# A coupled-map lattice on TensorE: six channels in groups of three with rings of 80 rows, regrouped into pairs with rings of 56 rows on two row tiles

## The chip, the cores and the metric

The kernel runs on one core of a Trainium2 chip. The metric is the device time of one execution in microseconds (us). All arithmetic concerned here is 32-bit floating point.

Words used below: *PE* or TensorE is the engine of matrix products, *DVE* is VectorE, *ACT* is ScalarE, *POOL* is GpSimd, *SP* is SyncE, which here only issues transfers. A *queue* is the list of instructions of one engine, which runs in order.

## The reference

Four layers, each of the form `x = x + f(group_norm(x))`, on 32 images of 8 channels and 256 x 256 pixels. The change concerns the first layer alone, and in it the map that is iterated 15 times:

```python
drive = x[:, :C_OUT]                       # all 8 channels, normalised
grid = drive
for _ in range(STEPS):                     # 15
    mapped = R * grid * (1.0 - grid)
    local = _conv(mapped, K_local, groups=C_OUT)      # 3x3, each channel by itself
    physics = (1.0 - EPS) * mapped + EPS * local
    grid = (1.0 - BETA) * physics + BETA * drive
cml_out = jnp.clip(grid, 0.0001, 1.0 - 0.0001)
h = jax.nn.relu(_conv(x, Wp, bp))                     # 3x3, 8 -> 128
nca_out = jax.nn.sigmoid(_conv(h, Wu, bu))            # 1x1, 128 -> 8
gin = jnp.concatenate([x, cml_out, nca_out], axis=1)
g = jax.nn.sigmoid(_conv(jax.nn.relu(_conv(gin, Wg1, bg1)), Wg2, bg2))
return g * cml_out + (1.0 - g) * nca_out
```

Layers 2 to 4 are a quantised 3x3 convolution, a 3x3 convolution and a 5x5 box filter; nothing of them is changed.

## The kernel before, in words

**Stages.** The first layer takes the first 13.6 ms of the span, one image (*batch*) after another. Layers 2 to 4 are pipelined over the batches in the rest.

**The map.** Six of the eight channels are iterated on TensorE, the other two on VectorE. For TensorE an image is cut into 32 x 16 patches of 8 columns by 16 rows. The 128 pixels of a patch lie on the 128 partitions, and the 512 patches lie along the free axis. So one step of a channel is one product with a 128 x 128 matrix (`patch_sb`, L391: all neighbours inside the patch) plus one product for the neighbours that lie in other patches: the *ring*. The table `RINGS` tells which pixels of which neighbouring patch are needed. The function `spread` (L250) copies those rows of the state, shifted by one patch, into the tile `rings`, and a second product (`ring_sb`, L393) adds their part in the same accumulator. The ring has 80 rows: 16 for the left side, 16 for the right, and 24 for the top and 24 for the bottom (8 pixels times three patches, the patches to the left and right included, of which most weights are zero).

**A step, in halves.** The channels are in two halves of three (`HALF`), each with its own tile of states and of rings. A half is: three patch products (L391), three ring products (L393), then on VectorE three additions of the drive in the accumulator (L402, 128 x 512), and on ScalarE three squares (L419) that write the new state; then `spread` issues four transfers on SP's queue (L259), which write `rings` for the next step. The accumulators come from a pool `ps_c` of three buffers of 512 columns, so a patch product has to wait until the square three products earlier has read its buffer.

**The two channels on VectorE.** Their image lies in `strip`; `tap` (L338) is one multiply-add of 128 x 1024 elements, nine of them a step: three in the first half, six in the second, followed by a maximum (L412) and the map itself (L413), which writes `strip`. Then `edges` copies the rows that neighbouring partitions need, with two transfers on SP's queue (L263, L264). VectorE's queue is in order, so a half's additions stand behind the taps of the half before.

**What lies between.** The rest of the layer (the hidden convolution, and the gate) for the batch before is a generator, `gated` (L487), whose pieces are put between the pieces of the map by hand. `lattice` yields a number at each place where other work may stand, and the main loop (L664 to L671) draws pieces of `gated` until their own numbers have used it up. A piece may be a product `ph` (L633) with its ReLU on ScalarE (L638), a group of four products `pn` (L610, each 32 columns wide, on column tiles), or gate products (L531, L539, L543, L548). Behind a gate's products come seven operations on VectorE (L561 to L568). A half yields 1.7 after its additions and taps, then issues squares and transfers, and yields `BLOCK - 1.7`, with `BLOCK = 6.3`. The statistics and the loads of the next batch come from a third generator, `errands` (L266), one piece a half; its transfers and those of `gated` are on POOL's queue. The first batch has no batch before it, so its steps have no such work between. All queues keep the order in which the program is written (`manual_schedule`).

Of the kernel before, what the change touches and what calls it, by code (L numbers as in the profile page):

```python
# [9 lines left out]
F32 = mybir.dt.float32  # L10
BF16 = mybir.dt.bfloat16
AF = mybir.ActivationFunctionType
ALU = mybir.AluOpType
# [4 lines left out]
P = 128  # L18
# [3 lines left out]
RB = H // HB  # L22
# [14 lines left out]
RINGS = (  # L37
    (0, 16, PW - 1, PW, -SY, 1, 0),
    (16, 16, 0, PW, SY, 1, 0),
    (32, 8, (RB - 1) * PW, 1, -1 - SY, 3, SY),  # L40
    (56, 8, 0, 1, 1 - SY, 3, SY),
)
RING = 80


CP = 6
HALF = CP // 2
RQ = 4
BLOCK = 6.3
STEPS = 15  # L50
R_, EPS_, BETA_ = 3.9, 0.3, 0.15

# [8 lines left out]
def window(ap, offset, dims):  # L61

    return bass.AP(ap.tensor, ap.offset + offset, [list(d) for d in dims])
# [3 lines left out]
def kernel(  # L67
# [10 lines left out]
    def const(pool, src, shape, name):  # L78
        t = pool.tile(shape, F32, name=name)
        nc.sync.dma_start(t, src)  # L80
        return t
# [86 lines left out]
    with ExitStack() as es:  # L168
# [6 lines left out]
        psum = es.enter_context(tc.tile_pool(name="ps_a", bufs=3, space=PSUM))  # L175

        patch_sb = const(wt, patch, [P, CP, P], "patch_sb")
        ring_sb = const(wt, ring, [RING, CP, P], "ring_sb")
        taps_sb = const(wt, taps, [P, 9], "taps_sb")
        kern_sb = const(wt, kern, [P, CP, 9], "kern_sb")  # L180
        pick_sb = const(wt, pick, [P, P], "pick_sb")
# [37 lines left out]
        d2s = [wt.tile([P, RQ, W], F32, name=f"d2_{i}") for i in range(2)]  # L219
        nh = wt.tile([P, 8, WP], F32, name="nh")  # L220
        zero = wt.tile([C, WP], F32, name="zero")
        states = [wt.tile([P, HALF, SN], F32, name=f"state{i}") for i in range(2)]
        rings = [wt.tile([RING, HALF, SN], F32, name=f"rings{i}") for i in range(2)]
        flat = wt.tile([P, NPX], F32, name="flat")
        acc = wt.tile([P, RQ, W], F32, name="acc")
        sts = [[wt.tile([P, 2], F32, name=f"st{j}_{i}") for j in range(2)] for i in range(2)]
        strip = wt.tile([P, RQ + 2, WP], F32, name="strip")
        for t in (*xbs, nh, zero, strip):
            nc.gpsimd.memset(t, 0.0)
        for t in (*states, *rings):  # L230
            nc.gpsimd.memset(t, 0.25)


# [11 lines left out]

        def inner(c):

            return states[c // HALF][:, c % HALF, AT : AT + TX * SY].rearrange("p (x y) -> p x y", y=SY)[:, :, 0:TY]

        def spread(half):  # L250

            long = (HALF - 1) * SN + RN
            state = states[half]
            row = state.ap[0][0]
            to = rings[half].rearrange("p c n -> p (c n)")
            for q, n, p, step, far, m, by in RINGS:
                at = p * row + AT + far
                dims = [[step * row, n]] + ([[by, m]] if m > 1 else []) + [[1, long]]
                nc.sync.dma_start(to[q : q + n * m, 0:long], window(state, at, dims))  # L259

        def edges():

# [65 lines left out]
        def lattice(b, ahead):  # L328
# [8 lines left out]
            def tap(dy, dx):  # L337
                nc.vector.scalar_tensor_tensor(  # L338
                    acc, strip[:, dy : dy + RQ, dx : dx + W],
                    taps_sb[:, 3 * dy + dx : 3 * dy + dx + 1],  # L340
                    d2 if dy == 1 and dx == 0 else acc, ALU.mult, ALU.add,
                )
# [27 lines left out]
                    edges()  # L370
                yield 1
            dr = flat.rearrange("p (x c y) -> p c x y", x=TX, c=C)
            for c in range(CP):
                nc.scalar.activation(inner(c), dr[:, c], AF.Square, bias=minus)
                nc.scalar.activation(
                    dr[:, c], dr[:, c], AF.Identity, bias=lift[:, c : c + 1], scale=BETA_
                )
                if c == 0:
                    nc.scalar.mul(d2, d2, BETA_)
                if c % HALF == HALF - 1:  # L380
                    spread(c // HALF)
                yield 1.5
            yield 4
            for step in range(STEPS):
                for half in range(2):
                    mine = range(HALF * half, HALF * half + HALF)
                    pss = []
                    for c in mine:
                        ps = ps_c.tile([P, 512], F32, name="psc")
                        pss.append(ps.rearrange("p (x y) -> p x y", y=TY))  # L390
                        nc.tensor.matmul(pss[-1], patch_sb[:, c, :], inner(c), start=True, stop=False)  # L391
                    for c in mine:
                        nc.tensor.matmul(  # L393
                            pss[c % HALF], ring_sb[:, c, :],
                            rings[half][:, c % HALF, 0 : TX * SY].rearrange(
                                "p (x y) -> p x y", y=SY
                            )[:, :, 0:TY],
                            start=False, stop=True,
                        )
                    for c in mine:  # L400
                        ps = pss[c % HALF]
                        nc.vector.scalar_tensor_tensor(ps, ps, FLOOR, dr[:, c], ALU.max, ALU.add)  # L402
                    if step == STEPS - 1:
                        for c in mine:
                            nc.vector.tensor_scalar(
                                dr[:, c], pss[c % HALF], 0.0001, 1.0 - 0.0001, ALU.max, ALU.min
                            )
                    for dy in (1,) if half == 0 else (0, 2):
                        for dx in range(3):
                            tap(dy, dx)  # L410
                    if half == 1 and step < STEPS - 1:
                        nc.vector.tensor_scalar(acc, acc, FLOOR, None, ALU.max)  # L412
                        nc.vector.scalar_tensor_tensor(own, acc, 1.0, acc, ALU.subtract, ALU.mult)  # L413
                    if half == 1 and step == STEPS - 1:
                        nc.vector.tensor_scalar(own, acc, 0.0001, 1.0 - 0.0001, ALU.max, ALU.min)
                    yield 1.7
                    if step < STEPS - 1:
                        for c in mine:
                            nc.scalar.activation(inner(c), pss[c % HALF], AF.Square, bias=minus)  # L419
                        spread(half)  # L420
                        if half == 1:
                            edges()
                    next(ahead, None)
                    yield BLOCK - 1.7
            for t4 in range(TX // 4):
                ps = psum.tile([P, 512], F32, name="ps")
                for j in range(4):
# [481 lines left out]
def laid_out(inputs):  # L909
# [6 lines left out]
    w3h = np.zeros((72, 2, P), f)  # L916
    k5 = inputs["L3_conv_weight"][0, 0]
    patch = np.zeros((P, CP, P), f)
    ring = np.zeros((RING, CP, P), f)
    for m in rows:  # L920
        for dy in range(3):
            for dx in range(3):
                y, x = m // PW + dy - 1, m % PW + dx - 1
                far = (-SY if x < 0 else SY if x >= PW else 0) + (-1 if y < 0 else y >= RB)
                p = y % RB * PW + x % PW
                if far == 0:
                    patch[p, :, m] = K[:CP, 0, dy, dx]
                for q, n, p0, step, far0, count, by in RINGS:
                    for j in range(count):
                        i, off = divmod(p - p0, step)  # L930
                        if far0 + j * by == far and off == 0 and 0 <= i < n:
                            ring[q + i * count + j, :, m] = K[:CP, 0, dy, dx]
    for dy in range(5):
        for m in rows:
            k = m + dy - 2
# [107 lines left out]
```

## Time and profile before

| | us |
|---|---|
| median of 3 runs (16277.27 to 16305.33) | 16303.53 |
| the profiled execution | 16318.33 |
| its span, first to last instruction | 16316.6 |

| engine, share of the span busy | |
|---|---|
| TensorE products (42888) | 95% |
| TensorE weight loads | 38% |
| VectorE | 72% |
| ScalarE | 35% |
| GpSimd | 34% |
| mean granted clock of TensorE | 0.961 |

| group | count | mean of one |
|---|---|---|
| L391 patch product, 128 x 512 | 5760 records | 626 ns |
| L393 ring product, 80 rows, 512 columns | 5760 records | 607 ns |
| L402 addition on VectorE | 2880 | 696 ns |
| L338 tap on VectorE | 4320 | 1284 ns (with `acc`), 1277 ns (with `d`) |
| L413 the map on VectorE | 448 | about 1227 ns |
| L419 square on ScalarE | 2688 | 690 ns |
| L259 ring transfer of 159.5 KB, and of 106.3 KB | 1920 each | |
| L263, L264 transfers of `strip`, 126 KB | 960 | |

How to read it. A product of 32-bit numbers is two records of TensorE, one after the other, each with its own weight load; so 5760 records are 2880 products (32 batches x 15 steps x 6 channels). Records overlap in time, so their mean length is more than what each one costs; the distance from start to start tells the cost. The DMA engines are busy for 67% between the first and the last batch of the first layer, VectorE for 76%.

### The profile page before, as it was taken

The page shows a single profiled execution, that of the slowest core. Times are in us where ns is not written, and L with a number is a line of the kernel's source. Part 1 is how long each engine was busy: PE and PEld are TensorE (multiplying, and loading weights), DVE is VectorE, ACT ScalarE, POOL GpSimd, SP SyncE. Part 2 cuts the span into 40 slices and gives each one's busy share as a digit, 9 for nine tenths or more (in the row PEclk, how much of TensorE's full clock was granted, in tenths as well). Part 3 has the DMA queues.
Part 4 walks back from the last instruction along what each step waited for, and adds up shares of the span by engine and source line. Part 5 has one row for each costly group of instructions (what it writes and reads, how often), then busy time and mean ns, then how long its engine had stood idle before and what let it go on. Part 6 is the DMA issues. An engine that isn't in the chain of part 4 may idle for free.

```text
span 16316.6 us, 141125 instructions
## 1 busy us (share of the span) xinstructions
PE 15452.2 (95%) x42888; PEld 6215.7 (38%) x42888; DVE 11705.9 (72%) x14652; ACT 5726.7 (35%) x8862; POOL 5598.2 (34%) x9491
## 2 busy tenths in 40 slices
PE   6999999999999999999999999999999997999999
PEld 2333333333333333333333333333333332333333
DVE  7777777777777777777777777777777764555554
ACT  2433444443434434443434444343444442111110
POOL 1333333333333333333333333333333342111111
PEclk7999999999999999999999999999999998999999
DMA  4766666666666666666666666666666664555554
GB/s 104 148 146 144 150 147 144 147 150 146 149 144 148 150 147 147 144 147 145 147 142 149 148 144 147 141 148 146 147 149 147 146 134 98 119 119 119 119 118 105
DMA packets 1057742, 2276.12 MB, mean 139 GB/s; under 512 B 419740, under 2 KB 623508, under 8 KB 1050724
## 3 DMA queue, kind: packets, MB, share of 16 engines
q0 software_dynamic: 704512, 1492.80, 40.6%
q1 hardware_dynamic: 352484, 774.29, 23.4%
q8 instruction: 356, 5.83, 0.2%
q14 instruction: 390, 3.19, 0.1%
HBM read 1078.04 MB, written 471.38 MB: 95 GB/s over the span
## 4 chain that ended last, share of the span: by engine, by line
PE 74%; DVE 13%; DMA 7%; ACT 3%; issue 2%; SPq 1%; POOL 0%; DVEq 0%; ACTq 0%; POOLq 0%
PE ph L633 17%; PE psc L391 14%; PE psc L393 13%; PE pg L531 9%; DVE acc L338 7%; PE psv L725 5%; PE pn L610 5%; PE psv L811 4%; DMA qb<-qh 3%; DMA rings<-state 2%; PE psv L729 2%; PE pq L548 1%; PE pg L543 1%; PE pg L539 1%; DVE psc L402 1%
## 5 line engine op out<-in xcount | busy, mean ns | idle before, releaser
L338 DVE SCALAR_TENSOR_TENSOR acc<-strip,taps_sb,acc 128x1024 f32<-128x1024 f32 x3840 | 4930.4, 1284 | 124.8 <-DMA strip<-strip 4.7
L505 POOL DMA_DIRECT2D im<-xn_d x6144 | 3458.3, 566 | 3250.0 <-PE ph L633 1434.7
L633 PE MATMUL ph<-im,wp_sb 72*128 72x512 f32 x8192 | 4091.7, 615 | 308.8 <-ACT hh L638 251.3
L638 ACT ACTIVATE hh<-ph,bp_sb 128x512 f32<-128x512 f32 x4096 | 2755.8, 690 | 4441.9 <-PE ph L633 4385.7
L402 DVE SCALAR_TENSOR_TENSOR psc<-psc,flat 128x512 f32<-128x512 f32 x2880 | 1921.4, 696 | 2813.0 <-PE psc L393 2797.2
L391 PE MATMUL psc<-state,patch_sb 128*128 128x512 f32 x5760 | 2812.0, 626 | 74.1 <-ACT state L419 63.3
L393 PE MATMUL psc<-rings,ring_sb 80*128 80x512 f32 x5760 | 2713.5, 607 | 129.8 <-DMA rings<-state 129.8
L633 PEld LDWEIGHTS ph<-im,wp_sb 72*128 72x128 f32 x8192 | 1489.5, 193 | 2425.4 <-issue 1587.8
L419 ACT ACTIVATE state<-psc,minus 128x512 f32<-128x512 f32 x2688 | 1690.2, 690 | 1818.8 <-DVE psc L402 1713.1
L391 PEld LDWEIGHTS psc<-state,patch_sb 128*128 128x128 f32 x5760 | 1114.5, 199 | 1696.2 <-issue 1375.7
L393 PEld LDWEIGHTS psc<-rings,ring_sb 80*128 80x128 f32 x5760 | 1114.7, 194 | 1576.8 <-issue 1545.7
L569 POOL DMA_DIRECT2D x_d<-xc x256 | 146.9, 574 | 3493.1 <-DVE xc L564 3416.6
L811 PE MATMUL psv<-xr,w_sb 128*128 128x512 f32 x2560 | 1162.9, 600 | 1.3 <-DVE xr L792 1.3
L610 PE MATMUL pn<-hh,wu_sb 128*32 128x512 f32 x8192 | 1133.9, 609 | 3.3 <-ACT hh L638 3.3
L776 POOL DMA_DIRECT2D x_d<-x x512 | 321.0, 643 | 1941.0 <-DVE x L770 1696.3
L725 PE MATMUL psv<-xh,w_sb 128*128 128x512 f32 x1536 | 753.0, 629 | 9.6 <-issue 9.6
L531 PE MATMUL pg<-xq,wg_sb 128*128 128x512 f32 x1536 | 749.3, 626 | 0.0
L754 ACT ACTIVATE x<-psv,b_sb,sc 128x512 f32<-128x512 f32 x256 | 199.3, 779 | 1466.2 <-PE psv L729 1465.8
L531 PE MATMUL pg<-cq,wg_sb 128*128 128x512 f32 x1536 | 713.7, 601 | 0.0
L811 PEld LDWEIGHTS psv<-xr,w_sb 128*128 128x128 f32 x2560 | 466.1, 189 | 610.8 <-issue 606.0
L338 DVE SCALAR_TENSOR_TENSOR acc<-strip,taps_sb,d 128x1024 f32<-128x1024 f32 x480 | 613.2, 1277 | 0.0
L831 DVE TENSOR_TENSOR y<-psv,y 128x512 f32<-128x512 f32 x256 | 177.1, 692 | 593.7 <-PE psv L811 593.7
(163 smaller groups left out, 12188.9 us busy)
## 6 DMA issues: line engine op xcount, KB each, us to landing
im<-xn_d POOLq DMA_DIRECT2D x6144, 96.6 KB, 6.6
rings<-state SPq DMA_DIRECT2D x1920, 159.5 KB
rings<-state SPq DMA_DIRECT2D x1920, 106.3 KB
strip<-strip SPq DMA_DIRECT2D x960, 126.0 KB
xn_d<-xb POOLq DMA_DIRECT2D x128, 516.0 KB, 7.7
nr_d<-xb POOLq DMA_DIRECT2D x128, 516.0 KB, 7.2
xq<-nr_d POOLq DMA_DIRECT2D x128, 516.0 KB, 5.1
cq<-cr_d POOLq DMA_DIRECT2D x128, 516.0 KB, 7.9
```

What stands on the lines that cost most here:

```text
L338: nc.vector.scalar_tensor_tensor(acc, strip[:, dy : dy + RQ, dx : dx + W], taps_sb[:, 3 * dy + dx : 3 * dy + dx + 1], d2 if dy == 1 and dx ...
L391: nc.tensor.matmul(pss[-1], patch_sb[:, c, :], inner(c), start=True, stop=False)
L393: nc.tensor.matmul(pss[c % HALF], ring_sb[:, c, :], rings[half][:, c % HALF, 0 : TX * SY].rearrange("p (x y) -> p x y", y=SY)[:, :, 0:TY], ...
L402: nc.vector.scalar_tensor_tensor(ps, ps, FLOOR, dr[:, c], ALU.max, ALU.add)
L419: nc.scalar.activation(inner(c), pss[c % HALF], AF.Square, bias=minus)
L505: nc.gpsimd.dma_start(im[24 * dy : 24 * dy + 24, k, 0:run], window(xn_d[b % 3], at, [[HP * WP, C], [1, 3], [1, run]]),)
L531: nc.tensor.matmul(o, wg1_sb[:, s, dx, :], src[:, :, dx : dx + W], start=s == dx == 0, stop=False,)
L610: nc.tensor.matmul(pn[32 * q : 32 * q + 32, :], wu_sb[:, i, :], hh, start=i == 0, stop=i == 3,)
L633: nc.tensor.matmul(ph.rearrange("p (k w) -> p k w", w=W), wp_sb, im[:, :, j * WP : j * WP + W], start=True, stop=True,)
L638: nc.scalar.activation(hh, ph, AF.Relu, bias=bp_sb)
L725: nc.tensor.matmul(o, w[:, dx, :], src[:, 2 * i : 2 * i + 2, dx : dx + W], start=dx == 0, stop=False,)
L811: nc.tensor.matmul(pss[k].rearrange("p (c w) -> p c w", w=W), w3_sb[:, dx, :], xr[:, k, mine, dx : dx + W], start=dx == 0, stop=stop,)
```

## The change

The six channels are taken in three pairs, (0, 3), (1, 4), (2, 5), in place of two halves of three. The ring shrinks to 56 rows: 16 for each side, 8 for the top and 8 for the bottom, and 4 for two corners above and 4 for two corners below, copied by transfers of their own. The ring of a pair's first channel lies on partitions 0 to 55, that of its second on 64 to 119, so that its two ring products work on different halves of the rows of TensorE's array (in the built program, both stand as tiles of 64 rows by 128 columns). Six transfers now serve each channel side. Pairs 0 and 1 share one set of states and rings, pair 2 has its own: `spread` is called after pair 1 for the first set (12 transfers of rows of 1122 elements) and after pair 2 for the second (12 of rows of 543 elements).

The taps are dealt out 2, 2 and 5. The third pair is followed by the maximum and the map of `strip`, then by `edges`. Yields are 0.8 and 0.8 after each of the first two pairs, and 0.8 and 8.6 after the third: 12.6 a step, as before. Pieces of `errands` come after pairs 0 and 2. The accumulator pool keeps its three buffers.

```diff
 RINGS = (
     (0, 16, PW - 1, PW, -SY, 1, 0),
     (16, 16, 0, PW, SY, 1, 0),
-    (32, 8, (RB - 1) * PW, 1, -1 - SY, 3, SY),
-    (56, 8, 0, 1, 1 - SY, 3, SY),
+    (32, 8, (RB - 1) * PW, 1, -1, 1, 0),
+    (40, 8, 0, 1, 1, 1, 0),
+    (48, 2, (RB - 1) * PW, PW - 1, -1 - SY, 2, 2 * SY),
+    (52, 2, 0, PW - 1, 1 - SY, 2, 2 * SY),
 )
-RING = 80
+RING = 56
+LOW, HIGH = 0, 64
...
-HALF = CP // 2
+PAIRS = CP // 2
+SETS = ((0, 2), (2, 1))
...
-BLOCK = 6.3
+BLOCK = 12.6
...
-        states = [wt.tile([P, HALF, SN], F32, name=f"state{i}") for i in range(2)]
-        rings = [wt.tile([RING, HALF, SN], F32, name=f"rings{i}") for i in range(2)]
+        states = [
+            [wt.tile([P, k, SN], F32, name=f"state{i}_{side}") for side in range(2)]
+            for i, (_, k) in enumerate(SETS)
+        ]
+        rings = [wt.tile([P, k, SN], F32, name=f"rings{i}") for i, (_, k) in enumerate(SETS)]
...
+        def spread(i):
+
+            long = (SETS[i][1] - 1) * SN + RN
+            to = rings[i].rearrange("p c n -> p (c n)")
+            for state, base in zip(states[i], (LOW, HIGH)):
+                row = state.ap[0][0]
+                for q, n, p, step, far, m, by in RINGS:
+                    at = p * row + AT + far
+                    dims = [[step * row, n]] + ([[by, m]] if m > 1 else []) + [[1, long]]
+                    nc.sync.dma_start(
+                        to[base + q : base + q + n * m, 0:long], window(state, at, dims)
+                    )
...
-            for c in range(CP):
+            for c in (0, 3, 1, 4, 2, 5):
                 nc.scalar.activation(inner(c), dr[:, c], AF.Square, bias=minus)
...
-                if c % HALF == HALF - 1:
-                    spread(c // HALF)
+                if c >= PAIRS + 1:
+                    spread(c - PAIRS - 1)
                 yield 1.5
             yield 4
+            taps_of = (((1, 0), (1, 1)), ((1, 2), (0, 0)), ((0, 1), (0, 2), (2, 0), (2, 1), (2, 2)))
             for step in range(STEPS):
-                for half in range(2):
-                    mine = range(HALF * half, HALF * half + HALF)
+                for j in range(PAIRS):
+                    i = j // 2
+                    mine = (j, PAIRS + j)
                     pss = []
                     for c in mine:
                         ps = ps_c.tile([P, 512], F32, name="psc")
                         pss.append(ps.rearrange("p (x y) -> p x y", y=TY))
                         nc.tensor.matmul(pss[-1], patch_sb[:, c, :], inner(c), start=True, stop=False)
-                    for c in mine:
+                    for ps, base in zip(pss, (LOW, HIGH)):
                         nc.tensor.matmul(
-                            pss[c % HALF], ring_sb[:, c, :],
-                            rings[half][:, c % HALF, 0 : TX * SY].rearrange(
+                            ps, ring_sb[base : base + RING, j, :],
+                            rings[i][base : base + RING, j - SETS[i][0], 0 : TX * SY].rearrange(
                                 "p (x y) -> p x y", y=SY
                             )[:, :, 0:TY],
                             start=False, stop=True,
                         )
...
-                    for dy in (1,) if half == 0 else (0, 2):
-                        for dx in range(3):
-                            tap(dy, dx)
...
+                    for dy, dx in taps_of[j]:
+                        tap(dy, dx)
+                    end = j == PAIRS - 1
...
-                    yield 1.7
+                    yield 0.8
                     if step < STEPS - 1:
-                        for c in mine:
-                            nc.scalar.activation(inner(c), pss[c % HALF], AF.Square, bias=minus)
-                        spread(half)
-                        if half == 1:
+                        for c, ps in zip(mine, pss):
+                            nc.scalar.activation(inner(c), ps, AF.Square, bias=minus)
+                        if j == SETS[i][0] + SETS[i][1] - 1:
+                            spread(i)
+                        if end:
                             edges()
-                    next(ahead, None)
-                    yield BLOCK - 1.7
+                    if j != 1:
+                        next(ahead, None)
+                    yield BLOCK - 4.0 if end else 0.8
```

In the changed program the patch products stand at L409, the ring products at L411, the additions at L419, the taps at L352, the squares at L436 and the ring transfers at L271.

## The prediction, made blind

> **What bounds the kernel now.** I read the page's busy shares first, then its groups, the waits of TensorE, and the timeline of one step.
>
> ```profile
> PE 15452.2 (95%) x42888; PEld 6215.7 (38%) x42888; DVE 11705.9 (72%) x14652; ACT 5726.7 (35%) x8862; POOL 5598.2 (34%) x9491
> ...
> L391 PE MATMUL psc<-state,patch_sb 128*128 128x512 f32 x5760 | 2812.0, 626 | 74.1 <-ACT state L419 63.3
> L393 PE MATMUL psc<-rings,ring_sb 80*128 80x512 f32 x5760 | 2713.5, 607 | 129.8 <-DMA rings<-state 129.8
> ```
>
> TensorE is busy for 95% of the span and hardly waits for `psc` or rings: it is the bound. Each f32 product is two records. In unbroken rows they start 0.429 us apart, so a product costs 0.858 us. First to last ring product of a batch is 359.3 us (mean of 31 batches, trace), 29 half-steps and one group of 2.7 us: 24.6 us a step. The step's 12 map products are 10.3 us of it.
>
> What TensorE waits for today (line waited for: total, times, longest):
>
> ```profile
> PE ph L633 <- ACT hh L638: 251.3, 122, 4.9
> PE psc L393 <- DMA rings<-state: 129.8, 37, 18.9
> PE psc L391 <- ACT state L419: 63.3, 12, 7.3
> ```
>
> The first is VectorE running late: ScalarE's square waits for VectorE's addition, and the ReLUs queued behind it free TensorE's buffers late. The timeline shows such a wait and what follows it (start, length, idle before); the second view sums the 6 us after it (busy time by engine, then the clock, 0.68):
>
> ```profile
> 8250.71 1.12 PE L633 MATMUL ph<-im,wp_sb 72*128 72x512 f32 x2
> 8256.35 2.08 PE L633 MATMUL ph<-im,wp_sb 72*128 72x512 f32 x2 [4.51 <-ACT hh L638]
> 8258.22 3.73 PE L391 MATMUL psc<-state,patch_sb 128*128 128x512 f32 x6
> ```
>
> ```profile
> 8256.40:8262.40 6.00, 6.00 (x10) 2.74 (x11) 0.90 (x1) 1.74 (x3) 3.35 (x7) 0.68 1.05 171
> ```
>
> 4.5 us idle, then records 0.85 us apart. The granted clock is 0.5 for 6.83 us there, which costs another 3.4 us. Idle stretches of 1.9 us and more set this off in the trace; 0.8 us alone does not. The same pair of waits (3.15 and 4.51 us) comes back in nearly every batch, two windows with them: 14.5 us a batch.
>
> **What the skill says.** TensorEngine Tiling (Array Packing), "Key Properties": tiles run independently, with their own weight loads, and changing the mode drains the engine. The trace agrees, for column tiles:
>
> ```profile
> 7999.72 0.59 PE L393 MATMUL psc<-rings,ring_sb 80*128 80x512 f32 x1
> 8000.24 0.62 PE L539 MATMUL pg<-above,wgh_sb 72*32 72x512 f32 x1
> 8000.24 0.62 PE L539 MATMUL pg<-below,wgh_sb 72*32 72x512 f32 x1
> 8000.69 0.59 PE L539 MATMUL pg<-above,wgh_sb 72*32 72x512 f32 x1
> 8000.70 0.59 PE L539 MATMUL pg<-below,wgh_sb 72*32 72x512 f32 x1
> 8001.22 1.13 PE L543 MATMUL pg<-nh,wg_sb 128*128 128x512 f32 x2
> ```
>
> Two products run side by side. Entering costs 0.520 instead of 0.429 us, leaving 0.522. A weight load that isn't hidden adds its time less 0.08: 0.025 for 32 columns (0.106 us), 0.105 for 128 (0.186 us). No row tile is in this trace. TensorE: Matmul & The Clock Gate, Part 1, says that idle time halves the clock over windows of about 3.4 us: the trace agrees (0.5 for 3.41 to 20.5 us at a time). DMA: Bandwidth & Descriptors, on how many engines a transfer uses: the largest divisor up to 16, lowest-numbered first. So 16 rows use 16 engines, 8 rows 8, the new corners (2x2) two; the trace names no engine.
>
> **The change, part by part.**
>
> *Ring products.* Before: 4 records x 0.429 = 1.716 us a pair. After: in 0.091 + 0.105, two records side by side 0.858, out 0.093 + 0.105: 1.252. Saved 0.464 x 1440 pairs = **668 us**. If the new weight load cost as little as the column tiles', 783. If the two tiles' loads ran one after the other (+0.19), 395. If nothing ran side by side, a loss of 0.394 x 1440 = 567. I take 668, since the loads of column tiles overlap. The 2880 patch products, the 2880 additions (L402), the taps and squares keep their number and shape.
>
> *The order of a step.* The three buffers of `psc` used to serve three channels at a time, with 6.3 of other work (in the kernel's units) between; now pairs follow with about 1.6 us of other work between, and the second patch of pair 1 (then of pair 2) needs the buffer whose square of the pair before must be done. From the end of pair 0's TensorE slot: addition starts +0.23, takes 0.70, square 0.72: 1.7 us. TensorE gets there after 0.96 + G1 (G1: other products between the pairs, from the order of the changed program). Wait = 0.74 + VectorE's lateness - G1. After pair 2 VectorE owes 2 additions (1.3), 5 taps (5 x 1.32), 0.73 and 1.14: 9.8 us. A gate (seven operations, 4.76 us at 8034.61) follows in 6 of 15 steps, once it stands after pair 0; two statistics (0.84) in others. TensorE's way to the next addition is G3 + 2.96, G3 being 8.2 to 10.9. So a gate step leaves VectorE 0.7 to 3.3 us late. Worked down the 15 steps the waits are 1.71, 1.40, 3.50 (the gate after pair 0), 0.74, 0.74, 2.20, 1.45, 0.94, 2.30, 0.74 and 1.40 us (the other steps none) = 17.1 a batch. Three are over 1.9 us: three half-clock windows, 10.2. Cover that hid this before: 7.1 us between halves.
>
> *Before's two waits* belong to the old order and go: -14.5. What is late next is the `psc` wait just priced.
>
> *Ring transfers.* 8 of 6.8 KB rows become 24 of 4.5 and 2.2 KB rows; bytes a step fall from 1089 to 746 KB. SP issues one in 0.55 to 0.75 us:
>
> ```profile
> L259 SPq DMA_DIRECT2D rings<-state x3840: 549/727/3873, 47.5 to 13302.7; - x192
> ```
>
> So 12 take 8.1 us where 4 took 2.7, and SP is occupied 24 x 0.67 + 1.65 = 17.8 us of a step (7.3 before). First issue to last landing of a group of four is 10.8 us in the median, 12.6 at the third quartile, 13.7 at nine in ten (landings from the semaphores' records); undisturbed 8.5. The busiest engines carry 8 packets of 6.8 KB at about 0.8 us (7 packets in 5.6 us). Corners on the lowest two make 16 of 4.5 KB there, 0.53 each: 2.1 + 8.5 = 10.6 undisturbed, 1.9 more, so 12.7, 14.5 and 15.6. The first set has 14.0 to 14.4 us (it had 18): about 0.3 us a step, partly while VectorE is late anyway: 2 a batch. Every transfer also waits for the one eight before it; at 7 us in flight (measured mean) 26 take 22.8 us of a step, just inside. Queued behind are the second set (needed 25 us after the first issue, lands at about 20) and the edges of `strip`, which tap (0,0) of the next pair 1 needs; due about 23 against 25: nothing, while that cover holds, else VectorE stops. On POOL's queue the errands' transfers still come two a step, and the gated ones in the same number: nothing.
>
> *First rings of a batch.* Cover shorter by one yield (1.7), landing 1.9 later: 3.7.
>
> *First batch, setup:* VectorE-bound at 20 us a step, no gated work: nothing.
>
> Sum a batch: 17.1 + 10.2 - 14.5 + 2 + 3.7 = 18.5; x 31 = 574. Net 668 - 574 = 94. The profiled execution took 16,318 (span 16,317): 16,224. It lies 15 above the median of the runs, so **16,210**.
>
> **Rivals.**
> A, this forecast: own range 16,095 to 16,315 (783 instead of 668; or one window more, 3.4 x 31 = 105).
> B, the waits are mostly hidden: half the `psc` wait (8.5), one window, no ring wait: 8.5 + 3.4 - 14.5 + 3.7 = 1, so 31: 637 less, 15,670. For it: ScalarE is idle 65%, and half-clock windows give VectorE time. Against: gate steps carry 14.6 us of VectorE work into an opening of 12.
> C, slower: **the ring products of pair 0 wait for their rings.** Place: L411 on `rings`. If a foreign packet delays each ring packet (0.29), not the transfer once, the busiest engine ends at 2.1 + 16 x 0.82 = 15.3 in the median, 1.1 us a step, 16 a batch; a third of it hides late VectorE; a window more: 14. 16.5 + 14 = 30.5 a batch, 945: 277 slower, 16,580. It decides from 5 us a batch, 0.33 a step (668/31 = 21.5 less 16.5). For it: 18 us of SP issue and 14 us of opening. Against: fewer bytes.
> D, the row tiles don't run side by side (the change doesn't do what it says): +567 and half of the waits, 287: 17,160. Against: column tiles do.
>
> **Chances.** A 0.36, B 0.21, C 0.33, D 0.10. 0.2% (33 us) is about what a measurement of this kernel can tell from no change: A is 0.28 faster, 0.07 same, 0.01 slower; C 0.32 slower, 0.01 same. Faster 0.49, same 0.08, slower 0.43. The range leaves out D and less than half of B: 15,650 (half of B) to 16,840 (C with a second window, 105, and none of its ring waits hidden, 155).
>
> **What would show it.** Right: two L411 records with one start; a pair's slot near 1.25; waits of L409 on squares (L436) near 17 us a batch; more half-clock windows, mean clock under 0.961. Wrong: L411 records 0.43 apart (D); waits on `rings` above 5 us a batch (C); waits of VectorE on `strip`, which I price at nothing; L409 waits under 8 us a batch (B).

## The result, and the profile after

The changed kernel takes 16,541 us (median; 16,529 to 16,550), the kernel before 16,298 (16,277 to 16,305): a ratio of 1.0153, interval 1.0140 to 1.0166. It is 1.5% slower, where 16,210 and a gain of 0.5% had been forecast. The profiled executions span 16,527.2 and 16,316.6 us.

On the page of the changed kernel, the same lines as before (busy time, groups):

```profile
PE 15208.5 (92%) x42888; PEld 5498.6 (33%) x42888; DVE 11615.9 (70%) x14652; ACT 5801.6 (35%) x8862; POOL 5597.2 (34%) x9493
...
L409 PE MATMUL psc<-state,patch_sb 128*128 128x512 f32 x5760 | 3045.6, 640 | 433.9 <-ACT state L436 384.4
L411 PE MATMUL psc<-rings,ring_sb 56*128 56x512 f32 x5760 | 1915.3, 673 | 429.5 <-DMA rings<-state 415.3
```

The ring products' busy time fell from 2713.5 to 1915.3 us: the row tiles work. But TensorE's share fell from 95% to 92%, and the idle time ahead of the two groups rose from 74 and 130 us to 434 and 430. The waits of TensorE (line waited for: total, times, longest):

```profile
PE psc L411 <- DMA rings<-state: 415.3, 162, 15.4
PE psc L409 <- ACT state L436: 384.4, 367, 5.1
PE ps L109 <- DVE mv L106: 145.6, 35, 28.1
...
PE ph L652 <- ACT hh L657: 18.3, 34, 2.6
```

Compare with before: the ReLU wait of 251 us is gone, as forecast. The squares' wait has come in its place, as forecast. Waits on rings tripled. The wait of the statistics product L109 is nearly new: before, that product (L104 there) waited five times, 47.9 us in all. VectorE waits on the strip's edges:

```profile
DVE acc L352 <- DMA strip<-strip: 129.9, 55, 7.0
```

It was 4.7 us before. One wait on rings and what follows it show the mechanism. The first view is TensorE's timeline (start, length, idle before), the second SP's, the third sums stretches of 6 us (five engines' busy time, then the granted clock):

```profile
8751.77 1.12 PE L411 MATMUL psc<-rings,ring_sb 56*128 56x512 f32 x2
8756.78 2.04 PE L411 MATMUL psc<-rings,ring_sb 56*128 56x512 f32 x2 [3.89 <-DMA rings<-state]
8758.75 0.58 PE L109 MATMUL ps<-mv,gavg_sb 128*128 128x1 f32 x2
```

```profile
8737.61 22.78 SPq L271 DMA_DIRECT2D rings<-state  x24
```

```profile
8757.00:8763.00 6.00, 6.00 (x9) 2.43 (x10) 3.71 (x7) 1.38 (x2) 2.65 (x5) 0.50 0.52 136
8763.00:8769.00 6.00, 6.00 (x19) 1.52 (x19) 3.15 (x4) 2.14 (x4) 0.00 (x0) 0.88 0.05 16
```

SP begins the 24 ring transfers at 8737.61. TensorE's two products of the lower tile have their rings at 8751.77, those of the upper tile get theirs at 8756.78, 19.2 us after the first issue. After the 3.89 us of idle time the clock is at half for all of the next 6 us: another 3 us. TensorE does 9 records there, and 19 in the 6 us after.

**Where the time went, as a sum.** For each kernel I took the mean of the 30 fully gated batches from one first map of `strip` to the next (trace), TensorE's idle stretches over 0.1 us, and the time at clock 0.5, which costs half of itself (records are 0.85 us apart there, 0.43 at full clock). What is left is the time in which TensorE worked. In us a batch:

| kernel | batch | waits | on rings | on squares | half clock | rest |
|---|---|---|---|---|---|---|
| before | 418.2 | 14.5 | 3.3 | 0 | 27.6 | 389.9 |
| changed | 425.4 | 29.6 | 11.1 | 12.1 | 44.4 | 373.6 |

"Rest" is batch - waits - half clock / 2. The change is -16.3 of work, +15.1 of waits, +8.4 of half clock: +7.2, and 30 x 7.2 = 216 of the spans' 211. The forecast's own terms were -21.5 (668 / 31), waits 17.1 + 2 + 3.7 - 7.66 = +15.1, and one half-clock window more, +3.4. That the total of the waits is as forecast is luck, since its parts are not; work and clock are 5 us each worse. That is 10 us a batch, 310 of the 331 us that the forecast missed by.

(Squares' waits of before, 63 us in all, lie outside these batches.)

The ring waits of a batch do not lie evenly. Of 11.2 us (all 31 gated batches), 5.9 are at step 0 (3.2 before), 1.6 at step 2 and 3.2 at step 11. From first issue to last landing a first set takes 9.8 to 10.1 us in six of the 15 groups of a batch (median of each) and 12 to 18.4 in the others: 16.4, 15.7 and 18.4 for steps 0, 2 and 11. (The set of step 6 takes 18.4 as well, but TensorE asks for it only 18.9 us after the first issue; for steps 0, 2 and 11 it asks after 9.3, 13.7 and 14.2.) The trace shows what is different there. While SP issues the 12 transfers for one of the six quiet steps, GpSimd issues one or none in five of the six (median), and SP takes 8.1 us. While SP issues those for steps 0, 2 and 11, GpSimd issues 10 or 11, and SP takes 11.2, 11.0 and 12.2 us, mostly because some of its transfers now have to wait for the one eight before. Over all groups the landing is 12.0 in the median, 15.8 at the third quartile and 17.9 at nine in ten, where the forecast had 12.7, 14.5 and 15.6: the median was right and the tail was not.

### The profile page after: what moved, and what is told of

Same layout as the page of the kernel before. It is cut to its first block, busy times and chain, and to the rows that moved or that the text cites. A ratio compares the mean times of both kernels' runs of the same rounds, so it can differ in the third digit from the quotient of the medians.

```text
span 16527.2 us, 158466 instructions
## 1 busy us (share of the span) xinstructions
PE 15208.5 (92%) x42888; PEld 5498.6 (33%) x42888; DVE 11615.9 (70%) x14652; ACT 5801.6 (35%) x8862; POOL 5597.2 (34%) x9493
## 4 chain that ended last, share of the span: by engine, by line
PE 56%; DVE 19%; DMA 15%; SPq 3%; ACT 3%; issue 3%; POOL 0%; ACTq 0%; DVEq 0%; POOLq 0%
PE ph L652 14%; DMA rings<-state 10%; PE psc L409 10%; DVE acc L352 8%; PE psc L411 7%; PE pg L550 6%; PE psv L744 5%; PE psv L830 4%; PE pn L629 4%; DMA qb<-qh 3%; SPq L271 3%; DVE psc L419 3%; ACT state L436 2%; PE psv L748 2%; DMA strip<-strip 1%
## 5 line engine op out<-in xcount | busy, mean ns | idle before, releaser
L352 DVE SCALAR_TENSOR_TENSOR acc<-strip,taps_sb,acc 128x1024 f32<-128x1024 f32 x3840 | 4923.9, 1282 | 230.7 <-DMA strip<-strip 129.9
L652 PE MATMUL ph<-im,wp_sb 72*128 72x512 f32 x8192 | 4257.2, 634 | 37.4 <-ACT gt L569 19.0
L657 ACT ACTIVATE hh<-ph,bp_sb 128x512 f32<-128x512 f32 x4096 | 2794.5, 687 | 3994.0 <-PE ph L652 3931.3
L419 DVE SCALAR_TENSOR_TENSOR psc<-psc,flat 128x512 f32<-128x512 f32 x2880 | 1875.2, 693 | 2988.8 <-PE psc L411 2981.5
L409 PE MATMUL psc<-state,patch_sb 128*128 128x512 f32 x5760 | 3045.6, 640 | 433.9 <-ACT state L436 384.4
L436 ACT ACTIVATE state<-psc,minus 128x512 f32<-128x512 f32 x2688 | 1720.9, 688 | 3044.6 <-DVE psc L419 2682.3
L411 PE MATMUL psc<-rings,ring_sb 56*128 56x512 f32 x5760 | 1915.3, 673 | 429.5 <-DMA rings<-state 415.3
L652 PEld LDWEIGHTS ph<-im,wp_sb 72*128 72x128 f32 x8192 | 1443.2, 195 | 2449.5 <-issue 2109.0
L409 PEld LDWEIGHTS psc<-state,patch_sb 128*128 128x128 f32 x5760 | 1069.9, 200 | 2272.8 <-issue 1221.1
L411 PEld LDWEIGHTS psc<-rings,ring_sb 56*128 56x128 f32 x5760 | 506.4, 193 | 1710.6 <-issue 1208.8
L499 POOL DMA_DIRECT2D below<-nh x288 | 194.4, 675 | 1353.9 <-ACT nh L607 1333.1
L352 DVE SCALAR_TENSOR_TENSOR acc<-strip,taps_sb,d 128x1024 f32<-128x1024 f32 x480 | 612.0, 1275 | 0.0
```

Of the source, the lines that this page charges most:

```text
L352: nc.vector.scalar_tensor_tensor(acc, strip[:, dy : dy + RQ, dx : dx + W], taps_sb[:, 3 * dy + dx : 3 * dy + dx + 1], d2 if dy == 1 and dx ...
L411: nc.tensor.matmul(ps, ring_sb[base : base + RING, j, :], rings[i][base : base + RING, j - SETS[i][0], 0 : TX * SY].rearrange("p (x y) -> ...
L436: nc.scalar.activation(inner(c), ps, AF.Square, bias=minus)
L652: nc.tensor.matmul(ph.rearrange("p (k w) -> p k w", w=W), wp_sb, im[:, :, j * WP : j * WP + W], start=True, stop=True,)
L657: nc.scalar.activation(hh, ph, AF.Relu, bias=bp_sb)
```

## The experiments

My theory after the result: the row tiles save what was said; the time goes to rings that land late in a few steps, because SP has 12 transfers a set to issue, and every wait that this makes is doubled by the half clock. Rivals: late VectorE is the true cause (five taps after the last pair, gate work), and the ring wait only covers it; or the corners' bytes, which the forecast puts on few DMA engines, delay all rings. All ratios are to the kernel before, with 95% intervals.

**Row tiles taken out.** Zero weights fill up each product to 128 rows:

```diff
...
-ps, ring_sb[base : base + RING, j, :],
-rings[i][base : base + RING, j - SETS[i][0], 0 : TX * SY]
+ps, ring_sb[:, j + PAIRS * (base == HIGH), :],
+rings[i][:, j - SETS[i][0], 0 : TX * SY]
...
```

> The changed kernel with its order, transfers and pairs, but each ring product is taken over all 128 rows of the array, with zero weights on the other channel's rows, so that no product stands on a row tile. Theory (the row tiles save what they were priced at, 0.47 us a pair, and the new order gives it back): slower than the changed kernel by most of 0.47 x 1440 = 678 us, less what the longer step hides of the waits: 16,900 to 17,200. Rival (changing the mode of the array costs as much as running side by side gains): 16,541 as the changed kernel, or less. Rival (all is bound by the landing of the rings, and TensorE's time is hidden): 16,541 to 16,650.

16,689 us, 1.0238 (1.0216 to 1.0261): 148 more than the changed kernel: less than the theory had (16,900 at least), more than the rivals (16,650 at most). The rest rises by 17.2 us a batch, but with the longer step the squares' wait falls from 12.1 to 6.0 and the half clock from 44.4 to 26.5, while the ring waits rise from 11.1 to 17.6. The saving is in the records, and most of it is spent on waiting and on the clock. Why more waiting on rings comes with less half clock here stays open.

**Sets of one and two pairs**, so that pair 0's rings leave earlier:

```diff
-SETS = ((0, 2), (2, 1))
+SETS = ((0, 1), (1, 2))
...
```

> The changed kernel with pair 0 alone in the first set of states and rings, and pairs 1 and 2 in the second. So the transfers of the first set start a pair earlier, and the second set is first needed by pair 1, one gap later. Theory (waits for rings and for the edges of strip, 11 and 4 us a batch, come from 24 issues in a row on SP's queue against 14 us of opening): the wait of L411 on rings falls from 11 to 6 us a batch or less, that of VectorE on strip from 130 us in all to under 40, with some half-clock windows gone: 150 to 300 us faster than the changed kernel, 16,240 to 16,390. Rival (the waits for squares alone decide): 16,500 to 16,541.

16,561, 1.0163 (1.0140 to 1.0187): a miss. The ring wait moved from pair 0 (10.7 us a batch to 2.0) to pair 1 (none to 11.0). VectorE's waits on the strip fell from 129.9 to 7.7 us in all, and that gave nothing here. What costs is the set, wherever it is needed.

**Fewer taps after the last pair:**

```diff
-((1, 2), (0, 0)), ((0, 1), (0, 2), (2, 0), (2, 1), (2, 2)))
+((1, 2), (0, 0), (0, 1)), ((0, 2), (2, 0), (2, 1), (2, 2)))
```

> The changed kernel with one tap moved from pair 2 to pair 1 (2, 3 and 4 taps in place of 2, 2 and 5), which fills a stretch of about 1.7 us in which VectorE waits for the ring products of pair 2. Theory (a gate step finds VectorE late, and the second patch of pair 1 waits for its square): VectorE is 1.3 us less late in the 6 gate steps of a batch, so the wait of L409 on squares falls from 13.4 to about 7 us a batch and one or two half-clock windows with it: 200 to 350 us faster than the changed kernel, 16,190 to 16,340. Rival (rings decide): the ring wait takes the place, 16,480 to 16,541.

16,383, 1.0050 (1.0035 to 1.0066): 158 less, short of the 200 to 350 expected. Squares' wait 12.1 to 9.1, the statistics' 3.4 to 2.1. Late VectorE is a real term, but a small one.

**One more piece of other work ahead of the statistics product L109:**

```diff
-for _ in stats_parts(psum, bn, st, gavr_sb, "ps"):
+for k, _ in enumerate(stats_parts(psum, bn, st, gavr_sb, "ps")):
     yield 0
+    if k == 0:
+        yield 0
```

> The changed kernel with the first statistics product of a gated batch drawn one piece later. In the changed kernel it waits 3.4 us in TensorE's queue for VectorE once a batch (29 of 31), and a half-clock window follows. Theory (each such wait costs its own time and half of the window after it): 3.4 + 3.4 to 5 us a batch, 150 to 260 us faster than the changed kernel: 16,280 to 16,390. Rival (the wait moves to the next product, or hides another wait, as the rings): 16,480 to 16,541.

16,351, 1.0028 (1.0019 to 1.0038): 190 less. The wait that the forecast had overlooked (3.4 us a batch; VectorE finishes a gate late, and L109 is next in TensorE's order) is gone, and the half clock falls by 8.2 us, which is 4.1 more. The two edits together:

> Two edits that moved the time alone are put together: taps 2, 3 and 4 after the pairs instead of 2, 2 and 5 (alone -158 us), and one more piece of other work between the statistics and the product that takes them (alone -190 us). If they act at different places the sum holds: 16,190, between 16,160 and 16,250, faster than the kernel before by 0.5%. If the statistics' wait was the same VectorE lateness that the taps remove, the gains overlap by a third or more: 16,280 to 16,350, no faster than before.

16,281, 0.9991 (0.9983 to 1.0000): 261 of the 348 us of the sum. Ring waits stay at 12.2 us a batch.

**The ring wait taken away, the transfers kept.** The products read a tile that isn't written:

```diff
...
-rings[i][base : base + RING, j - SETS[i][0], 0 : TX * SY].rearrange(
+still[base : base + RING, :].rearrange(
```

> The ring products read a third tile that nothing writes after setup, so no ring product can wait for its rings; the 24 ring transfers a step are still issued and land where nobody reads (left out: the neighbours' values). Theory 1 (the ring wait is a path of its own: 11.2 us a batch in the changed kernel, 5.9 at step 0, 1.1 at step 2, 3.2 at step 11, with one or two half-clock windows after them): the waits on rings go to 0 and a third of them comes back as waits on the squares, 31 x (11.2 x 2/3 + 3.4) = 337 less than 16,541: 16,200, between 16,050 and 16,300. Theory 2 (VectorE is late in the same steps and takes the ring wait's place): waits on the squares rise by as much, 16,430 to 16,540.

16,168, 0.9919 (0.9903 to 0.9934): 373 less, as the first theory had it. But the squares' wait rises from 12.1 to 16.2 us a batch, and without any ring wait 33.3 of the 44.4 us at half clock stay. What keeps the gain from going further is, as I read it, the same queue: in that kernel VectorE waits 403.8 us on the strip and ScalarE 548.5 us to overwrite a state that a ring transfer has not read yet (changed kernel: 129.9 and 350.6; before: 4.7 and 85.4; with the corners on GpSimd, below, 7.5 and 21.8). SP's late queue has three customers, and TensorE's ring product is only the first.

**Fewer transfers.** Corners left out:

```diff
-for q, n, p, step, far, m, by in RINGS:
+for q, n, p, step, far, m, by in RINGS[:4]:
```

> The eight corner transfers of a step are not issued, 16 instead of 24 (left out: the diagonal neighbours at the corners of a patch, whose rows keep their first value). Theory 1 (rings land late because SP has to issue 12 transfers a set and the last four wait for one of the first eight to land): a set lands in about 9 us in quiet steps and 12 in busy ones, waits on rings fall from 11.2 to 3 to 5 us a batch, VectorE's waits on the strip from 130 to under 20 us, time 16,541 - 31 x 7 x 2/3 - 31 x 3.4 = 16,290, between 16,230 and 16,400. Theory 2 (the DMA engines' other load at steps 0, 2 and 11 sets the landing, however few transfers there are): ring waits stay above 8 us a batch, 16,470 to 16,550.

15,730, 0.9658 (0.9644 to 0.9673): 812 less, three times what was expected. Sets land in 8.5 us in the median and 13.4 at nine in ten, ring waits are 0.9 us a batch, and the half clock falls from 44.4 to 17.1. Number or bytes? The same number of transfers, with 4 bytes of each corner row:

```diff
+some = 1 if m > 1 else long
...
-to[base + q : base + q + n * m, 0:long], window(state, at, dims)
+to[base + q : base + q + n * m, 0:some], window(state, at, dims)
```

> All 24 ring transfers of a step are issued, but each of the eight corner transfers carries 4 bytes of each of its four rows instead of 4.5 or 2.2 KB (left out: the rest of the corner rows, which keep their first value). Theory 1 (the number of transfers on SP's queue costs: 0.67 us of issue each, and the ninth to twelfth of a set wait for one of the first eight to land): nearly as slow as the changed kernel, ring waits above 7 us a batch, 16,350 to 16,560. Theory 2 (the corners' bytes, which all go through few engines, delay the other rows): as fast as without corners, 15,730 to 15,900, ring waits 1 to 3 us a batch.

16,355, 1.0031 (1.0018 to 1.0044): 187 of the 812. Sets still land at 11.3, 14.7 and 16.9 us (median, third quartile, nine in ten). About a quarter is bytes, three quarters are the transfers' number. In quiet groups the landing differs by 9.1 - 7.1 = 2.0 us, near the 2.7 of four issues; in step 11's group by 16.9 - 12.8 = 4.1, where a transfer also waits for the one eight before it.

The traces tell the two apart, for the landing. Undisturbed, SP issues a first set of 12 in 8.1 us and one of 8 in 5.3: four more transfers are 2.8 us in every group. What SP takes beyond that is 1.3 us on the mean in the changed kernel and 3.9 at nine in ten, against 0.3 and 0.9 without corners; 0.9 of the 1.3 is time in which the transfer eight before had not landed. In step 11's group it is 12.2 - 8.1 = 4.1 us. So the issue is the larger part of the mean, and the wait for an earlier transfer makes the tail.

**The same bytes on other queues.** Half of the rings with ScalarE:

```diff
-for state, base in zip(states[i], (LOW, HIGH)):
+for state, base, queue in zip(states[i], (LOW, HIGH), (nc.sync, nc.scalar)):
...
-nc.sync.dma_start(
+queue.dma_start(
```

> The twelve ring transfers of the upper half go out on ScalarE's queue, twelve stay with SP; bytes and rows are the same. Theory 1 (number of issues on SP and its chain of transfers set the landing): a set's last landing falls from 12.0 to about 8 to 9 us in the median, ring waits to 3 to 6 us a batch; ScalarE loses about 12 x 0.6 = 7 us a step, which the squares and the gated ReLUs behind it feel: 16,350 to 16,550. Theory 2 (other load on the engines sets it): landing and ring waits as they were, with ScalarE's delay on top: 16,600 to 16,900.

19,756, 1.2124 (1.2106 to 1.2142), worse than either theory. ScalarE's timeline shows six issues, then a ReLU that had to wait for them:

```profile
4008.73 4.08 ACTq L271 DMA_DIRECT2D rings<-state  x6
4012.85 1.26 ACT L657 ACTIVATE hh<-ph,bp_sb 128x512 f32<-128x512 f32 x2 [4.15 <-DMA rings<-state]
```

TensorE waits for such ReLUs 55 us a batch. Now only the corners, with GpSimd, whose queue already carries the gated part's loads:

```diff
-nc.sync.dma_start(
+(nc.sync if m == 1 else nc.gpsimd).dma_start(
```

> The eight corner transfers of a step go out on GpSimd's queue, sixteen stay with SP; all bytes are moved. Theory 1 (number of transfers on SP): most of what leaving the corners out gave comes back without leaving anything out, 15,800 to 16,100, ring waits 2 to 4 us a batch. Theory 2 (bytes on few engines): 16,400 to 16,560. Against both: GpSimd's queue is in order, a corner waits there for the squares, and the loads of the gated part wait behind it: then TensorE waits for those loads or for corners, and the time is over 16,600.

15,699, 0.9632 (0.9618 to 0.9647): 842 less than the changed kernel and 604 less than before, with nothing left out, and better than the first theory's expectation. By the run with 4 bytes a row, the corners' bytes account for about 187 of the 842; the rest is SP's shorter queue. Its waits, and GpSimd's busy share (34% before):

```profile
PE psc L409 <- ACT state L436: 399.5, 398, 5.0
PE ps L109 <- DVE mv L106: 148.3, 35, 28.7
...
PE psc L411 <- DMA rings<-state: 46.2, 36, 5.3
```

```profile
PE 14737.6 (94%) x42888; PEld 5356.1 (34%) x42888; DVE 11610.1 (74%) x14652; ACT 5789.4 (37%) x8862; POOL 7719.6 (49%) x13333
```

The squares' and the statistics' waits stand where they stood (399.5 and 148.3 us against 384.4 and 145.6). The ring wait is gone, 415 to 46, and with it most of the half clock, 44.4 to 15.9 us a batch. To see which waits had halved the clock, I looked for the longest idle time of TensorE in the 8 us before each stretch at clock 0.5 (stretches in the 30 batches, and us at half clock a batch; other waits, two stretches at most, are left out):

| longest wait before the stretch | before | changed | corners with GpSimd |
|---|---|---|---|
| of ring products | 27, 10.1 | 81, 23.0 | 6, 0.9 |
| on squares | 0 | 49, 13.2 | 31, 6.6 |
| of the statistics product | 0 | 29, 7.3 | 29, 7.3 |
| of `ph` | 89, 16.8 | 2, 0.7 | 2, 0.7 |

So the ring waits carried half of it, and squares and statistics the rest. The squares' mean of 1.0 us (399.5 / 398) hides two kinds: in the changed kernel none of the 252 under 1.5 us is followed by a half clock within 7 us, 11 of the 42 from 1.5 to 3 us are, and all 38 of 3 us or more.

**Edges ahead of the second set**, with taps 2, 3, 4 and late statistics:

```diff
+if end:
+    edges()
 if j == SETS[i][0] + SETS[i][1] - 1:
     spread(i)
-if end:
-    edges()
...
```

> On top of taps 2, 3, 4 and the late product of the statistics, the two transfers of the strip's edges are issued ahead of the second set's rings instead of behind them. The waits of VectorE on the strip (77 us in all with the other two edits, 130 in the changed kernel) should go: 16,281 - 77 = 16,200 if every microsecond of them is on the path, 16,280 if none is; 16,180 to 16,300. If the edges, which wait for the taps, hold the second set back so that pair 2 waits for its rings, over 16,320.

17,876, 1.0968 (1.0950 to 1.0987). The last case came true, far larger: the edges wait on SP for VectorE's last taps, and pair 2 then waits for its rings 17.9 us a batch. SP's timeline shows 24 ring transfers in a row behind the edges:

```profile
3309.25 0.86 SPq L277 DMA_DIRECT2D strip<-strip  x1
3310.16 0.80 SPq L278 DMA_DIRECT2D strip<-strip  x1
3311.07 19.88 SPq L271 DMA_DIRECT2D rings<-state  x24
```

**A fourth accumulator for the map**, two buffers for the gated part:

```diff
-name="ps_c", bufs=3
+name="ps_c", bufs=4
...
-name="ps_a", bufs=3
+name="ps_a", bufs=2
```

> The map gets a fourth buffer in PSUM, so that a pair's second patch product no longer waits for the square of the pair before; the gated part has two buffers instead of three. If the waits on the squares are a path of their own (13.4 us a batch, some 3 with a half-clock window after them): they fall below 2 us a batch, the ring waits stay, and the gated part's waits on its ReLUs come up by 3 to 6 us a batch: 16,541 - 31 x (11 + 3 - 5) = 16,260, between 16,150 and 16,420. If VectorE's lateness moves elsewhere (two buffers of the gated part wait for ReLUs behind late squares): 16,480 to 16,700.

16,752, 1.0278 (1.0262 to 1.0294). The squares' wait is gone from the step loop, and the gated part's came instead:

```profile
PE psc L411 <- DMA rings<-state: 461.9, 175, 14.6
PE ph L652 <- ACT hh L657: 285.0, 346, 3.4
```

The rival had the mechanism, though the time lies above its 16,700: the kernel has eight accumulators in all, and this only moves the wait.

**Row tiles taken out, rings in time.** The first experiment's edit on top of the corners with GpSimd:

> Corners on GpSimd's queue as in that run (15,699), and the ring products over all 128 rows with zero weights, so no row tiles: every pair is 0.47 us longer, 678 us in all. If the late rings were what hid two thirds of this in the changed kernel (where it moved the time by 148), the difference comes back now that they are gone: 15,699 + 500 to 680 = 16,200 to 16,380. If the longer step hides it as before: 15,830 to 15,950.

15,941, 0.9795 (0.9772 to 0.9818): 242 more than with row tiles. That is the second case (15,830 to 15,950), not the 500 to 680 more of the first: late rings had hidden little of the saving (148 there). The sum says what did:

| kernel | batch | waits | on rings | on squares | half clock | rest |
|---|---|---|---|---|---|---|
| corners with GpSimd | 398.8 | 18.4 | 0.7 | 11.4 | 15.9 | 372.4 |
| the same, no row tiles | 407.0 | 10.5 | 1.0 | 4.8 | 8.5 | 392.3 |

Row tiles take 19.9 us of work from a batch; 7.9 come back as waits (6.6 of them on squares), 3.7 as half clock. What is left is 8.2. Without row tiles the rest is 392.3 against 389.9 before: the order in pairs costs about 2.4 by itself.

**The best version** puts the corners with GpSimd, taps 2, 3, 4 and the late statistics product together:

> Corners on GpSimd's queue, taps 2, 3 and 4, and the late product of the statistics. With the rings in time each edit should give what it gave together before (-261) or, where the ring waits had covered part, up to 350: 15,350 to 15,440. If the statistics' wait had only been as long as it was because of the late rings, one edit falls away: 15,500 to 15,600.

15,386 us (15,368 to 15,403), 0.9451 (0.9431 to 0.9470): 5.5% faster than the kernel before. The two edits give 313 here and 261 with late rings: terms of their own. Half clock is 7.9 us a batch.

## Why the prediction was wrong, point by point

In us a batch, the forecast's terms beside what the two kernels' traces give (clock: half of the time at half clock, by the longest wait before it):

| term | forecast | measured |
|---|---|---|
| ring products, saved work | -21.5 | -16.3 |
| waits on squares (`psc`), their clock | 17.1 + 10.2 | 12.1 + 6.6 |
| waits on rings, their clock | 5.7 + 0 | 7.8 + 6.5 |
| before's waits of `ph`, their clock | -14.5 | -8.8 - 8.1 |
| wait of the statistics product, its clock | 0 | 3.4 + 3.7 |
| other | 0 | 0.3 |
| sum | -3.0 | +7.2 |

The rings are the step that failed most: 14.3 us a batch instead of 5.7. The statistics product was left out, and the saving came out smaller in the sum. The squares, priced 8.6 too high, balanced what the rings cost beyond their price; that was luck.

- **Ring products, 668 us: the mechanism was right, the size in the sum was not.** The slot of a pair shows the row tiles side by side: records of a pair start 6 to 7 ns apart, the way in is 0.522, the passes 0.527 apart, the way out 0.520. From the record before a pair's ring products to the record after them that is 1.583 us, against 5 x 0.429 = 2.145 without row tiles. An undisturbed pair saves 0.562, more than the forecast's 0.464: 25.3 us for the 45 pairs of a batch. TensorE's timeline, two pairs of records in 1.06 us:

```profile
8310.46 1.13 PE L411 MATMUL psc<-rings,ring_sb 56*128 56x512 f32 x4
8311.52 1.13 PE L652 MATMUL ph<-im,wp_sb 72*128 72x512 f32 x2
```

  As the Trainium skill says (TensorEngine Tiling (Array Packing), "Key Properties"), tiles run independently; this case shows it for row tiles in f32 too. The sum has only 16.3 of the 25.3. The order in pairs takes 2.4 of them. In 141 of the 1,350 pairs the records do not run side by side, mostly because one channel's rings land later than the other's. How the rest divides stays open.
- **The `psc` wait, 17.1 us a batch: mechanism right, a third too high.** 12.1 us on squares. It is also part of what a shorter slot pays back, as the row tiles' two experiments show.
- **Half-clock windows: wrong.** I charged three windows to `psc` waits and none to ring waits. The changed kernel has 5.4 a batch (before 3.9): 2.7 follow a ring wait (0.9 before), 1.6 a wait on squares and 1.0 the statistics product. The kernel with the corners on GpSimd has 2.3 left, nearly all behind squares and statistics. The ring waits' share is 23.0 us at half clock a batch, which costs 11.5, as much as the 11.1 of the waits themselves. The skill (TensorE: Matmul & The Clock Gate, Part 1) has a window of about 3.4 us; the stretches of these batches last 3.41 to 13.65 us, 8.2 on the mean (44.4 / 5.4).
- **Before's two ReLU waits, -14.5: right.** 8.2 us of `ph` waits on ReLUs fell to 0.6.
- **Ring transfers, 2 a batch, and first rings, 3.7: the step that failed.** The waits on rings rose by 7.8 instead of 5.7 (2.7 at step 0, 5.1 in the other steps), and their half clock, priced at nothing, added 6.5. The 7.8 passes the 5 us a batch from which rival C was to decide; its 16,580 was the nearest number, and its place, L411 in pair 0, was right. I added a fixed 1.9 us to the landing times of before, for bytes on the lowest engines. But a transfer more is not a shift: it adds its issue and, once the group passes eight, a wait on an earlier transfer; in the groups that meet GpSimd's loads that wait grows to 3 or 4 us. So the median came out near the forecast (12.0 against 12.7) and the tail did not (17.9 against 15.6).
- **Edges, nothing while the cover holds: the cover failed, the price seems to have stayed near nothing.** VectorE waited 129.9 us for the strip, but the kernel in which only 7.7 of it is left was no faster (sets of one and two).
- **Not in the forecast:** the statistics product's 3.4 us a batch, with 7.3 us at half clock behind it (3.7). Taking this wait away gave 190 us, 6.1 a batch. I had listed late VectorE after gates and looked only at who waits on `psc`.
- **Rival D fell, rival B was wrong in the kernel as built,** and its 15,670 is met by the corners on another queue (15,699) by chance, through another mechanism: the `psc` waits were not hidden, the ring waits were gone.

What stays open: how the three quarters of the 812 us that go with the number of transfers divide between SP's issue and the wait on the transfer eight before. The traces divide the landing, not the time; both left together in each run here.

## What to carry to other kernels

Cutting a copy into more transfers costs the queue's issue time for each, and where a group outgrows what may be under way together, its tail lengthens by more than its median; price the landing at nine in ten, with other loads running, against the opening. Charge a wait of 3 us or more twice, once for itself and once for the clock, and look at how long the single waits are, not at their mean; a saving on the bound engine is worth only what the next short wait leaves of it. Before giving a change up, move the added transfers to a queue with room whose engine has nothing urgent behind them.

## What the runs showed of the hardware that was not expected

- The queue matters more than the bytes. The skill's Trainium Kernel Development and Optimization, "Key Constraints", says that issuing from several engines saves only the sequencer's issue time, and Perfetto Trace Analysis, "DMA Optimizations", that balancing issue over engines may help. Here eight corner transfers a step moved from SP to GpSimd were worth 842 us; twelve moved to ScalarE cost 3,214, since issues hold up its activations (six of them for 4.08 us).
- Idle time cost double: in the changed kernel 23.0 us a batch at half clock, which cost 11.5, followed ring waits of 11.1 us. Short waits on squares did not do this: none of 252 under 1.5 us was followed by half clock.
- Two f32 row tiles of 56 rows ran side by side: 1.583 us instead of 2.145 from the record before to the record after, way in and out included.
- Leaving out 51 MB of 610 on SP's queue (corners) was worth 812 us; thinning the same transfers to 4 bytes a row, 187.
